# A fused four-stage kernel: the embedding product on four column groups, edge transfers in GpSimd's queue, and two coefficient loads earlier in SP's queue

## The chip, the core and the metric

The kernel runs on one core of a Trainium2 chip, as one program with one launch. The core has five engines that run side by side, each through its own instructions in order: TensorE (PE in the profile, PEld for its weight loads), VectorE (DVE), ScalarE (ACT), GpSimd (POOL) and SyncE (SP). SP, ScalarE and GpSimd can each issue DMA transfers (SPq, ACTq, POOLq in the trace). The metric is the time of one execution on the device in microseconds (us); lower is better. Before the change the median of three runs is 2675.97 us (2674.63 to 2677.31).

## What is computed

The input `x` is a batch of 8 matrices of 512 x 512 in float32. Four layers follow each other; the diff touches the first and the start of the second.

```python
# layer 0, per batch: a stencil with given coefficient grids
gradv_Af  = grad(A[0]*f, 0) + grad(A[1]*f, 1)
gradvv_Bf = grad2(B[0]*f, 0) + grad2(B[1]*f, 1) + grad(grad(B[2]*f, 1), 0) + grad(grad(B[2]*f, 0), 1)
x = max(f + (-gradv_Af + gradvv_Bf * 0.5) * dt, 0)
# layer 1: attention, 16 heads of 32, with an adaptive layer norm
emb = silu(sin_emb(timestep)) @ W_ada + b_ada          # [8, 512] @ [512, 1024]
scale, shift = split(emb, 2)
x = ln(x) * (1 + scale) + shift
q, k, v = x @ Wq + bq, x @ Wk + bk, x @ Wv + bv
scores = q / sqrt(32) @ k.T + attention_bias, masked; probs = softmax(scores)
x = x + (probs @ v) @ Wo + bo
x = x + ff(ln(x) * g2 + beta2)
# layer 2: per batch one of 8 experts (gelu MLP, residual, norm)
# layer 3: low-rank response with a gate
```

## The kernel before

**Stages.** `fused_kernel` builds the constants and the silu of the sine embedding `sc` (128 partitions, 4 chunks, 8 batches). Then `grid_stage` does layer 0 for the first batch alone. `attention_stage` loops over 8 batches x 4 chunks x 4 row blocks ("units"); while it attends over batch b it also does layer 0 of batch b + 1, in small steps that it spreads over the units (`grid_loads`, `grid_step`, `grid_early`). `mlp_stage` does the rest. Nearly every instruction is pinned (`keep_in_program_order`, called `pin`), so on each engine the order in the code is the order on the chip. A matrix of 512 rows lies as 128 partitions x 4 row blocks (R = 4).

**The first batch's grid stage.** SP loads A, B, `f` and the weights. VectorE makes the coefficient grids and products; PE adds them up with shifted identities (`zi`) into four PSUM accumulators `acc[r]`, one for each row block (called `l0_r`, tile `l`, L251). The first and last row of the matrix have their own formulas. They are computed apart, on 64 partitions, into `xe` (blocks of 16 partitions: side x batch, for all 8 batches). The six coefficient grids are stored to DRAM through GpSimd's queue (L405: `coef_q`, `e`, `g`, `c`, `a`, `b`, 1 MB each) so that later batches can load them.

**The tail of the grid stage**, which the change touches:
- `embed(ps)` (L138 to 148): the product of `W_ada` and `sc`. Each of the 8 output chunks takes 4 matmuls with a 128x128 block of `wada` as the stationary operand and 8 columns of `sc` moving. The result `pe` lies as [128, 8, 8].
- Four steps on VectorE (L248, called from L514) take `acc[r]` to `x[:, r]`, in the order r = 0, 3, 1, 2, each followed by a Relu on ScalarE (L515).
- `edges()` (L501 to 513) runs after the Relu of r = 3. It overwrites the first and the last row of `x` from `xe`, in four transfers: two for the first row on SP's queue and two for the last row on ScalarE's.
- Four transfers on ScalarE's queue (L520) store all of `xe` to DRAM as `xed`, for the later batches.
- `stats(1)`, `stats(2)`, `stats(0)`, `stats(3)` on VectorE (L523, L524): statistics by row block. Row block 0 holds the first row of the matrix, row block 3 the last. Then the inverse root on GpSimd (L532) and four normalising steps on VectorE (L535).
- `embed_out(pe)` (L157): adds the bias and gives `ada`, the scale and shift.

**The head of the attention stage** is written out by hand from L1119 on. SP's queue gets: the mask of row block 0 (`mask_in`, L588), `grid_loads(1, -2)` (the second batch's `f` as `gf`, L713 to L718, and two q coefficients, L706), the first unit's bias (two transfers of 512 KB, L995), `Wv`, `grid_loads(1, -1)` (coefficients e and c, 512 KB each, L706), the next mask, the second unit's bias, `Wo`. On PE come the transposes of the first batch (`x1_in`, tile `xtr`, L570), the first q and k blocks (`pq`, `pk`, L567), the first scores (`s`), the v blocks (`pv`), and from then on a mix of units. Between the units VectorE does the products of the second batch's stencil (`gv`, L689), the softmax maximum with the bias (`bt`, L1030), and the sum of `bo` (L581). GpSimd adds the mask to the bias (L1006). ScalarE does the exponentials (L1035).

**Completion counters.** The tile framework gives each DMA one of eight completion counters in turn. SP's and ScalarE's transfers share one set of eight, GpSimd's have another set. A transfer waits until the one that had its counter before, eight transfers back in the same set, has landed. So in SP's queue L588 waits for the first edge transfer, and L717 for the third store of `xed`.

Of the kernel before, what the change touches and what calls it, by code (L numbers as in the profile page):

```python
# [11 lines left out]
F32 = mybir.dt.float32  # L12
# [4 lines left out]
ALU = mybir.AluOpType  # L17
# [3 lines left out]
NB = 8  # L21
S = 512
D = 512
P = 128
# [5 lines left out]
KC = D // P  # L30
RK = 32
# [8 lines left out]
def fused_kernel(ctx: ExitStack, tc: tile.TileContext, a: dict):  # L40
    nc = tc.nc

    const = ctx.enter_context(tc.tile_pool(name="const", bufs=1))
    small = ctx.enter_context(tc.tile_pool(name="small", bufs=4))
# [3 lines left out]
    ident = const.tile([P, P], F32, name="ident")  # L48
    make_identity(nc, ident)
    mhalf = const.tile([P, R], F32, name="mhalf")  # L50
# [4 lines left out]
    ada = const.tile([P, 2 * KC, NB], F32, name="ada")  # L55
# [4 lines left out]
    def x_home(b):  # L60
        return xp.tile([P, R, D], F32, name=f"x{b}", tag=f"x{b % 4}", bufs=1)

    xt = {0: x_home(0)}
# [10 lines left out]
    def layernorm(dst, src, eps, tag, pin=lambda i: i):  # L74
# [17 lines left out]
    wada = [  # L92
        xp.tile([P, KC, D], F32, name=f"wada{h}", tag=f"x{2 + h}", bufs=1) for h in range(2)
    ]
# [14 lines left out]
    bada = ep.tile([P, 2 * KC], F32, name="bada")  # L109
# [18 lines left out]
    sc = ep.tile([P, KC, NB], F32, name="sc")  # L128
# [6 lines left out]
    nc.scalar.activation(sc[:, 2:4, :], ang, AF.Sin)  # L135
    nc.scalar.activation(sc, sc, AF.Silu)

    def embed(ps):  # L138

        pe = ps.tile([P, 2 * KC, NB], F32, name="pe")  # L140
        for m in range(2 * KC):
            o = (m % KC) * P
            for k in range(KC):
                tc.keep_in_program_order(
                    nc.tensor.matmul(  # L145
                        pe[:, m, :], lhsT=wada[m // KC][:, k, o : o + P], rhs=sc[:, k, :],
                        start=k == 0, stop=k == KC - 1,
                    )
                )
        return pe  # L150

    def embed_bias():
# [4 lines left out]
    def embed_out(pe):  # L157
        tc.keep_in_program_order(
            nc.vector.tensor_tensor(
                ada, pe, bada[:, :, None].to_broadcast([P, 2 * KC, NB]), ALU.add  # L160
            )
        )

    dram = ctx.enter_context(tc.tile_pool(name="x1_dram", bufs=1, space=bass.MemoryType.DRAM))
# [13 lines left out]
    def load_rows():  # L178
# [5 lines left out]
        nc.sync.dma_start(bo, a["bo"][None, :].to_broadcast([P, D]))  # L184

    grid = grid_stage(
        tc, a, const, small, dram, xt[0], mhalf, ident, load_wada, load_w, load_rows, embed,
        embed_bias, embed_out,
    )


# [29 lines left out]


def grid_stage(
    tc, a, const, small, dram, x, mhalf, ident, load_wada, load_w, load_rows, embed,
    embed_bias, embed_out,
):


# [12 lines left out]
    nc = tc.nc  # L241
    pin = tc.keep_in_program_order
# [10 lines left out]
    with ExitStack() as ctx:  # L253
        cp = ctx.enter_context(tc.tile_pool(name="coef", bufs=1))
        gp = ctx.enter_context(tc.tile_pool(name="edge", bufs=1))
        ps = ctx.enter_context(tc.tile_pool(name="l0_ps", bufs=1, space=PSUM))
# [14 lines left out]
        n, W = 2 * NB, 128  # L271
# [11 lines left out]
        with tc.tile_pool(name="raw", bufs=1) as rp:  # L283
            a0, b0, a1, b1 = (
                rp.tile([P, R, D], F32, name=k) for k in ("a0", "b0", "a1", "b1")
            )

            ec8 = rp.tile([N // NB, 12, W + 2], F32, name="ec8")
            sel8 = rp.tile([N // NB, N // NB, NB], F32, name="sel8")
            pin(nc.gpsimd.memset(ec8, 0.0))  # L290

            def edge_cols(k):
                lo, hi = max(0, W * k - 1), min(D, W * k + W + 1)
                return slice(lo, hi), slice(lo - W * k + 1, hi - W * k + 1)

            for i, k in enumerate(blocks):
                c, u = edge_cols(k)
                pin(nc.gpsimd.dma_start(ec8[2 * i : 2 * i + 2, :, u], a["edge_c"][:, :, c]))
            pin(
                nc.gpsimd.tensor_copy(  # L300
                    sel8, ident[0 : N // NB, 0 : N // NB, None].to_broadcast([N // NB, N // NB, NB])
                )
            )

            halves = slice(0, 2), slice(2, 4)
            for h in halves:
                rows_in(b1, a["B"][1], h)
                rows_in(a1, a["A"][1], h)
            rows_in(b0, a["B"][0])
            rows_in(a0, a["A"][0])  # L310
            rows_in(f, a["x"][0])
            rows_in(b2, a["B"][2])
            nc.sync.dma_start(gw, a["c_ghost"].to_broadcast([P, 16]))
            nc.sync.dma_start(dth, a["dt"][None, :].to_broadcast([P, NB]))
            load_wada()
            load_w("Wq", "Wk")
            load_rows()
            pin(nc.gpsimd.memset(zi, 0.0))
            pin(nc.gpsimd.tensor_copy(zi[:, 0, 1 : P + 1], ident))
            pin(nc.gpsimd.tensor_scalar_mul(zi[:, 1, 1 : P + 1], ident, -1.0))  # L320
            gate = small.tile([P, 1], F32, name="gate_e", tag="gate_e", bufs=1)
            pin(nc.gpsimd.tensor_tensor(gate, f[:, 0, 0:1], f[:, 0, 0:1], ALU.add))
            for i, k in enumerate(blocks):
                c, u = edge_cols(k)
                pin(nc.gpsimd.dma_start(fe[n * i : n * i + n, :, u], a["edge_f"][:, :, c]))

            for i in range(4):
                pec = ps.tile([N, 3, W + 2], F32, name=f"pec_{i}", tag="pec", bufs=2)
                mm(
                    pec, sel8.rearrange("q s b -> q (s b)"), ec8[:, 3 * i : 3 * i + 3, :],  # L330
                    True, True,
                )
                pin(nc.scalar.copy(ec[:, 3 * i : 3 * i + 3, :], pec))

            for h in halves:
                tt(ca[:, h, :], b1[:, h, :], a1[:, h, :], ALU.add)
                tt(cb[:, h, :], b1[:, h, :], a1[:, h, :], ALU.subtract)
            tt(cc, b0, b1, ALU.add)
            pin(nc.scalar.mul(cc, cc, -2.0))
            tt(ce, a0, b0, ALU.add)  # L340
            tt(cg, b0, a0, ALU.subtract)
            pin(nc.scalar.mul(b2, b2, 0.5))
# [34 lines left out]
        for i, (u, v) in enumerate(  # L377
            ((ga[:, :, 1:5], gb[:, :, 0:4]), (gb[:, :, 508:512], ga[:, :, 509:513]))
        ):
            for k, w in enumerate((u, v)):  # L380
                o = 8 * i + 4 * k
# [100 lines left out]
        for p, i in ends:  # L482
            cols = (slice(1, 5), slice(W - 3, W + 1))[i]
            for k in range(2):
                o = 8 * i + 4 * k
# [7 lines left out]
        xe = cp.tile([N, W], F32, name="xe")  # L493
        stt(xe, se, dte, fe[:, 0, C], ALU.mult, ALU.add)
        pin(nc.vector.tensor_scalar(xe, xe, 0.0, None, ALU.max))
        pe = embed(ps)
        embed_bias()
        pin(nc.vector.tensor_scalar(dth, dth, 0.5, None, ALU.mult))
        st = small.tile([P, R, 6], F32, name="ln0_st", tag="ln0_st", bufs=1)
        mv = small.tile([P, R, 2], F32, name="ln0_mv", tag="ln0_mv", bufs=1)  # L500
        def edges():  # L501
            for o, u, c in ((0, 3 * n, 0), (n, n, 2 * W)):
                for side, q_ in ((0, nc.sync), (1, nc.scalar)):
                    p, r = side * (P - 1), side * (R - 1)
                    e0 = o + side * NB
                    pin(
                        q_.dma_start(
                            x[p : p + 1, r, c : c + 2 * W].rearrange("o (b w) -> o b w", w=W),
                            xe[e0 : e0 + u + 1 : u, :],
                        )  # L510
                    )
# [5 lines left out]
                edges()  # L517
        xed = dram.tile([n, D], F32, name="xed")
        for i, k in enumerate(blocks):
            pin(nc.scalar.dma_start(xed[:, W * k : W * k + W], xe[n * i : n * i + n, :]))  # L520

        def stats(r):
            pin(nc.vector.bn_stats(st[:, r, :], x[:, r, :]))  # L523
            pin(nc.vector.bn_aggr(mv[:, r, :], st[:, r, :]))  # L524

        stats(1)
        stats(2)
        stats(0)
# [16 lines left out]
def attention_stage(  # L545
# [12 lines left out]
    nc = tc.nc  # L558
    with ExitStack() as ctx:
        wp = ctx.enter_context(tc.tile_pool(name="aw", bufs=1, reuse_waits="tile"))  # L560
        pp = ctx.enter_context(tc.tile_pool(name="ap", bufs=2, reuse_waits="tile"))
        ps = ctx.enter_context(tc.tile_pool(name="a_ps", bufs=1, space=PSUM, reuse_waits="tile"))

        pin = tc.keep_in_program_order
# [156 lines left out]
        def grid_loads(n, j):  # L721
            if j == -2:
                xt[n] = x_home(n)
                grid_f(n)
            for k, key, p in (
                (-2, "q", 0), (-2, "q", 1), (-1, "e", 0), (-1, "c", 0), (1, "g", 0), (2, "a", 0),
                (4, "b", 0), (4, "q", 2), (6, "e", 1), (7, "c", 1), (8, "g", 1), (9, "a", 1),
                (10, "b", 1),
            ):
                if j == k:  # L730
                    coef(n, key, p)
# [258 lines left out]
        def load_bias(b, c, r):  # L990
            for u in range(2):
                hp = 2 * c + u
                bt = pp.tile([P, 2, S], F32, name=f"bt_{b}_{r}_{hp}", tag="bt", bufs=8)
                pin(
                    nc.sync.dma_start(  # L995
                        bt,
                        a["bias"][b, 2 * hp : 2 * hp + 2].rearrange("h (p r) k -> r p h k", r=R)[r],
                    )
                )
                bias[b, c, r, u] = bt  # L1000
# [119 lines left out]
        n = len(units)  # L1120
        mask_in(0, 0)
        grid_loads(1, -2)
        load_bias(*units[0])
        load_w("Wv")
        grid_loads(1, -1)
        mask_in(0, 1)
        load_bias(*units[1])
        load_w("Wo")
# [949 lines left out]
```

## Time and profile before

| what | us |
|---|---|
| median of 3 runs (lowest, highest) | 2675.97 (2674.63, 2677.31) |
| the profiled execution | 2674.74 |
| its span, first to last instruction | 2673.0 |
| PE busy in 0 to 60 / 60 to 100 / 100 to 200 / 200 to 1000 / 1000 to 2673 | 42.52 / 39.22 / 95.39 / 799.51 / 1660.26 |
| embedding product, L145, on the chain that ended last | 9.52 |
| first transposes of the attention stage, `xtr`, start on that chain | 59.62 |
| first softmax step of the first unit on DVE (L1030) starts | 77.74 |

The profile is one execution taken by the hardware profiler; durations that are quoted from it belong to that execution. A timeline row gives start, length, engine, line, operation, output <- input, count, and in brackets how long the engine had been idle and what ended it. A DMA row shows when the transfer was issued, not when it landed. PE's busy time is no measure of distance from its peak, since matmuls are pipelined.

Small transfers and their times from issue to landing, in the profile's list of DMA issues: `fe` 5.6 and 5.3 us, `ec` 6.0 and 6.4, the 2 KB rows of `coef_q` 3.8, the 1 MB stores `coef_q` to `coef_b` 4.3 to 12.5 (all in GpSimd's queue). For SP's and ScalarE's queues it lists no such times.

### The profile page before, as it was taken

How to read it: one execution, taken by the hardware profiler on the slowest of the kernel's cores; microseconds unless marked ns; L12 is line 12 of the kernel's file. 1: busy time of each engine (PE TensorE's matmuls, PEld its weight loads, DVE VectorE, ACT ScalarE, POOL GpSimd, SP SyncE). 2: the span in 40 equal slices, each digit the busy share in tenths (PEclk: the TensorE clock that was granted, in tenths of full speed). 3: DMA queues.
4: the chain of work that ended last, by engine and by line, in shares of the span. 5: the costliest groups of instructions: out<-in, count | busy, mean ns of one | idle time of the engine just before them, and what ended most of it. 6: DMA issues, size and time to landing. Idle time of an engine off the chain costs nothing.

```text
span 2673.0 us, 39423 instructions
## 1 busy us (share of the span) xinstructions
PE 2636.9 (99%) x14182; PEld 1958.2 (73%) x14182; DVE 1885.6 (71%) x3444; ACT 1004.4 (38%) x2091; POOL 1479.3 (55%) x1091
## 2 busy tenths in 40 slices
PE   7999999999999999999999999999999999999998
PEld 4455555555555555888888888888888888888887
DVE  7888898888888656676656656656566676676675
ACT  2576767677777765211211211211111221221221
POOL 3456565556555654565566565655535545545543
PEclk9999999999999999999999999999999999999999
DMA  8775766666666554653544454445335445445331
GB/s 313 262 239 192 249 211 228 212 246 235 204 238 221 186 169 148 197 147 85 162 148 122 141 150 143 118 135 171 107 128 184 132 148 185 133 147 185 123 105 38
DMA packets 241760, 460.31 MB, mean 172 GB/s; under 512 B 33848, under 2 KB 77440, under 8 KB 232478
## 3 DMA queue, kind: packets, MB, share of 16 engines
q1 hardware_dynamic: 237754, 447.04, 49.3%
q0 software_dynamic: 3360, 10.68, 2.9%
q8 instruction: 113, 1.85, 0.3%
q14 instruction: 81, 0.66, 0.1%
q10 hardware_dynamic: 452, 0.07, 0.0%
HBM read 398.43 MB, written 55.09 MB: 170 GB/s over the span
## 4 chain that ended last, share of the span: by engine, by line
PE 96%; DVE 2%; DMA 1%; ACT 0%; issue 0%; SPq 0%; POOL 0%; DVEq 0%; POOLq 0%; ACTq 0%
PE u L1221 29%; PE y L1221 29%; PE tr L570 9%; PE s L567 6%; PE ctx L567 4%; PE pv L567 4%; PE o L567 4%; PE pk L567 4%; PE pq L567 4%; PE l L251 1%; PE xtr L570 1%; PE xb L570 1%; DVE bt L1030 0%; DMA a<-in_A 0%; PE po L1221 0%; PE pe L145 0%
## 5 line engine op out<-in xcount | busy, mean ns | idle before, releaser
L1006 POOL TENSOR_TENSOR bt<-bt,mk 128x1024 f32<-128x1024 f32 x256 | 541.0, 2138 | 70.4 <-DMA bt<-in_bias 63.6
L1221 PE MATMUL y<-wo,act 128*128 128x256 f32 x2560 | 566.3, 380 | 0.0
L1221 PEld LDWEIGHTS y<-wo,act 128*128 128x128 f32 x2560 | 484.5, 190 | 71.6 <-issue 6.7
L1035 ACT ACTIVATE bt<-bt,mn 128x512 f32<-128x512 f32 x512 | 365.7, 718 | 84.9 <-DVE mn L1030 84.8
L570 PEld LDWEIGHTS tr<-ident,bt 128*128 128x128 f32 x2048 | 229.5, 141 | 148.0 <-issue 100.6
L1030 DVE CUSTOM_DVE_ANT_0 bt<-s,bt 128x512 f32<-128x512 f32 x512 | 330.2, 683 | 3.8 <-PE s L567 3.6
L1221 PE MATMUL u<-bt,wi 128*128 128x256 f32 x1440 | 330.5, 379 | 0.0
L1227 DVE TENSOR_TENSOR act<-u,u 128x512 f32<-128x512 f32 x256 | 173.1, 683 | 200.7 <-PE u L1221 129.7
L1221 PEld LDWEIGHTS u<-bt,wi 128*128 128x128 f32 x1440 | 273.5, 190 | 37.2
L570 PE MATMUL tr<-ident,bt 128*128 128x128 f32 x2048 | 277.0, 278 | 6.1 <-DVE pt L1060 1.7
L1062 ACT COPY pt<-tr 128x512 f32<-128x512 f32 x368 | 203.9, 584 | 207.5 <-PE tr L570 202.2
L1221 PE MATMUL u<-tb,ws 128*128 128x256 f32 x1024 | 242.2, 379 | 0.0
L1221 PE MATMUL y<-t,s 128*128 128x256 f32 x1024 | 227.8, 380 | 0.0
L1230 POOL TENSOR_TENSOR t<-wo,t 128x512 f32<-128x512 f32 x64 | 107.4, 1701 | 203.0 <-PE y L1221 203.0
L1221 PEld LDWEIGHTS u<-tb,ws 128*128 128x128 f32 x1024 | 194.3, 190 | 26.6 <-DVE tb L1227 0.2
L1221 PEld LDWEIGHTS y<-t,s 128*128 128x128 f32 x1024 | 194.0, 190 | 26.1
L1060 DVE COPY pt<-tr 128x512 f32<-128x512 f32 x144 | 99.2, 689 | 139.9 <-PE tr L570 139.0
L1585 ACT ACTIVATE act<-act,b 128x512 f32<-128x512 f32 x128 | 82.9, 711 | 292.7 <-DVE act L1227 292.7
L1585 ACT ACTIVATE act<-act,bi 128x512 f32<-128x512 f32 x128 | 83.8, 712 | 282.6 <-DVE act L1227 282.6
L1604 ACT COPY u<-u 128x512 f32<-128x512 f32 x64 | 36.4, 569 | 393.8 <-PE u L1221 277.5
L1227 DVE TENSOR_TENSOR x<-y,x 128x512 f32<-128x512 f32 (+1 forms) x97 | 64.7, 680 | 153.9 <-PE y L1221 103.6
L1227 DVE TENSOR_TENSOR u<-u,u 128x512 f32<-128x512 f32 x192 | 130.9, 682 | 55.4 <-PE u L1221 55.3
(324 smaller groups left out, 4191.1 us busy)
## 6 DMA issues: line engine op xcount, KB each, us to landing
bt<-in_bias SPq DMA_DIRECT2D x256, 512.0 KB
wo<-in_W SPq DMA_DIRECT2D x32, 1024.0 KB
wi<-in_Wi SPq DMA_DIRECT2D x32, 1024.0 KB
wo<-in_Wo_e SPq DMA_DIRECT2D x32, 1024.0 KB
wi<-in_W SPq DMA_DIRECT2D x28, 1024.0 KB
td<-tt SPq DMA_DIRECT2D x22, 1024.0 KB
bt<-td SPq DMA_DIRECT2D x176, 128.0 KB
gq<-coef_q SPq DMA_DIRECT2D x21, 512.0 KB
```

The lines of the kernel that those rows point to most:

```text
L567: pin(nc.tensor.matmul(out, lhsT=lhsT, rhs=rhs, start=start, stop=stop))
L570: pin(nc.tensor.transpose(out, src, ident))
L1006: nc.gpsimd.tensor_tensor(bt, bt, mask[b, r][:, None, :].to_broadcast([P, 2, S]), ALU.add)
L1030: nc.vector.tensor_tensor_reduce(bt[:, i, :], ss[h], bt[:, i, :], -1.0, 3.0e38, ALU.add, ALU.min, mn)
L1035: nc.scalar.activation(bt[:, i, :], bt[:, i, :], AF.Exp, bias=mn, scale=-1.0, accum_out=sums[b, c][:, h, r : r + 1],)
L1060: pin(nc.vector.tensor_copy(pt[:, :, r % 2, :], tr))
L1062: pin(nc.scalar.copy(pt[:, :, r % 2, :], tr))
L1221: pin(nc.tensor.matmul(out, lhsT=lhsT, rhs=rhs, start=start, stop=stop))
L1227: pin(nc.vector.tensor_tensor(out, x, y, op))
L1230: pin(nc.gpsimd.tensor_tensor(out, x, y, op))
L1585: nc.scalar.activation(acts[g][:, k, :], acts[g][:, k, :], func, bias=bi[:, j : j + 1])
L1604: pin(nc.scalar.copy(u1, p[0]))
```

## The change

There are three parts.

1. The embedding product turns its operands round. `sc` is put into a zeroed tile `sp` of 32 columns for each chunk (8 of them used), which is the stationary operand. `W_ada` streams through as the moving operand in pieces of 256 columns, and the four pieces go to four groups of 32 output partitions. The result `rows` is [4 x 32, 256], with the batch along partitions; ScalarE copies it to SBUF, and PE turns it back with two transposes. `embed_out` reads the turned layout.
2. The two transfers of the last row (`edges()`, side 1) and the four stores of `xed` are issued by GpSimd instead of ScalarE.
3. In the attention stage's head, `grid_loads(1, -1)` (e and c coefficients) goes ahead of the first bias and `Wv`.

```diff
+    def embed_in(pool):
+        sp = pool.tile([P, KC, RK], F32, name="sp")
+        tc.keep_in_program_order(nc.gpsimd.memset(sp, 0.0))
+        tc.keep_in_program_order(nc.gpsimd.tensor_copy(sp[:, :, 0:NB], sc))
+        return sp
+
-    def embed(ps):
-        pe = ps.tile([P, 2 * KC, NB], F32, name="pe")
-        for m in range(2 * KC):
-            o = (m % KC) * P
-            for k in range(KC):
-                tc.keep_in_program_order(
-                    nc.tensor.matmul(
-                        pe[:, m, :], lhsT=wada[m // KC][:, k, o : o + P], rhs=sc[:, k, :],
-                        start=k == 0, stop=k == KC - 1,
-                    )
-                )
-        return pe
+    def embed(ps, sp):
+        pin = tc.keep_in_program_order
+        rows = ps.tile([P, 2 * P], F32, name="pe_rows", tag="pec", bufs=2)
+        for k in range(KC):
+            for j in range(4):
+                o = 2 * P * (j % 2)
+                pin(
+                    nc.tensor.matmul(
+                        rows[j * RK : (j + 1) * RK, :], lhsT=sp[:, k, :],
+                        rhs=wada[j // 2][:, k, o : o + 2 * P], start=k == 0, stop=k == KC - 1,
+                    )
+                )
+        return rows
+
+    def embed_turn(ps, pool, rows):
+        er = pool.tile([P, 2 * P], F32, name="pe_sb")
+        tc.keep_in_program_order(nc.scalar.copy(er, rows))
+        pe = ps.tile([P, 2, P], F32, name="pe", tag="pec", bufs=2)
+        for h in range(2):
+            tc.keep_in_program_order(
+                nc.tensor.transpose(pe[:, h, :], er[:, h * P : (h + 1) * P], ident)
+            )
         return pe
...
     def embed_out(pe):
         tc.keep_in_program_order(
             nc.vector.tensor_tensor(
-                ada, pe, bada[:, :, None].to_broadcast([P, 2 * KC, NB]), ALU.add
+                ada.rearrange("p (j h) b -> p j h b", h=2),
+                pe.rearrange("p h (j b) -> p j h b", j=4)[:, :, :, 0:NB],
+                bada.rearrange("p (j h) -> p j h", h=2)[:, :, :, None].to_broadcast([P, 4, 2, NB]),
+                ALU.add,
             )
         )
...
             pin(nc.gpsimd.tensor_scalar_mul(zi[:, 1, 1 : P + 1], ident, -1.0))
+            sp = embed_in(gp)
             gate = small.tile([P, 1], F32, name="gate_e", tag="gate_e", bufs=1)
...
-        pe = embed(ps)
+        pe = embed(ps, sp)
...
-                for side, q_ in ((0, nc.sync), (1, nc.scalar)):
+                for side, q_ in ((0, nc.sync), (1, nc.gpsimd)):
...
-            pin(nc.scalar.dma_start(xed[:, W * k : W * k + W], xe[n * i : n * i + n, :]))
+            pin(nc.gpsimd.dma_start(xed[:, W * k : W * k + W], xe[n * i : n * i + n, :]))
...
+        pe = embed_turn(ps, gp, pe)
         stats(1)
...
         grid_loads(1, -2)
+        grid_loads(1, -1)
         load_bias(*units[0])
         load_w("Wv")
-        grid_loads(1, -1)
         mask_in(0, 1)
```

More of the change, by code (lines that the diff above doesn't have):

```diff
@@ L186, in fused_kernel @@
     grid = grid_stage(
-        tc, a, const, small, dram, xt[0], mhalf, ident, load_wada, load_w, load_rows, embed,
-        embed_bias, embed_out,
+        tc, a, const, small, dram, xt[0], mhalf, ident, load_wada, load_w, load_rows, embed_in, embed,
+        embed_turn, embed_bias, embed_out,
     )
@@ L223, in grid_stage @@
 def grid_stage(
-    tc, a, const, small, dram, x, mhalf, ident, load_wada, load_w, load_rows, embed,
-    embed_bias, embed_out,
+    tc, a, const, small, dram, x, mhalf, ident, load_wada, load_w, load_rows, embed_in, embed,
+    embed_turn, embed_bias, embed_out,
 ):
```

## The prediction

> **What bounds the kernel now.** I read the page first: its busy shares, then the chain that ended last.
>
> ```profile
> span 2673.0 us, 39423 instructions
> PE 2636.9 (99%) x14182; PEld 1958.2 (73%) x14182; DVE 1885.6 (71%) x3444; ACT 1004.4 (38%) x2091; POOL 1479.3 (55%) x1091
> PE 96%; DVE 2%; DMA 1%; ACT 0%; issue 0%; SPq 0%; POOL 0%; DVEq 0%; POOLq 0%; ACTq 0%
> ```
>
> TensorE (PE) sets the end. Time is won or lost only where PE's start in some stretch moves, or where PE waits. Everything the diff touches lies in the first 100 us, so next comes the chain of waits from 46 to 75 us (start, length, what):
>
> ```profile
> 45.81 4.29 PE l L251 x10
> 50.11 9.52 PE pe L145 x64
> 59.62 3.51 PE xtr L570 x16
> 63.13 4.20 PE pq L567 x8
> 67.33 3.45 PE pk L567 x8
> 70.80 0.70 ACT kt L658
> 71.54 1.14 PE s L567 x8
> 72.68 2.34 PE pv L567 x5
> ```
>
> The embedding product (L145) stands on the chain with 9.52 us; the transposes of the first batch (xtr) follow at once. Third, the timeline of the same stretch, for what else xtr needs: the normalised x.
>
> ```profile
> 49.21 0.63 ACT L515 ACTIVATE x<-x 128x512 f32<-128x512 f32 x1 [0.23 <-DVE x L248]
> 49.88 1.81 ACTq L507 DMA_DIRECT2D x<-xe  x2
> 51.73 0.63 ACT L515 ACTIVATE x<-x 128x512 f32<-128x512 f32 x1 [1.88 <-DMA x<-xe]
> 52.39 0.69 DVE L523 BATCH_NORM_STATS2 ln_st<-x 128x6 f32<-128x512 f32 x1 [1.50 <-ACT x L515]
> 52.62 0.34 SPq L588 DMA_DIRECT2D mu<-in_mask  x1
> 54.82 0.67 DVE L523 BATCH_NORM_STATS2 ln_st<-x 128x6 f32<-128x512 f32 x1
> 57.09 1.92 DVE L535 TENSOR_SCALAR x<-x,ln_mv,ln_r 128x512 f32<-128x512 f32 x4 [1.17 <-POOL ln_r L532]
> 58.79 0.22 SPq L717 DMA_DIRECT2D gf<-in_x  x1
> ```
>
> x is normalised at 57.09 + 1.92 = 59.01, only 0.6 us before PE finishes the embedding. Two chains run side by side and almost tie; shortening one alone is worth 0.6.
>
> **The embedding product.** 64 instructions of 8 columns go. In come 16 matmuls of 32 output rows and 256 columns, two records each: exactly the form of ctx (L567), whose 32 records take 1.86 us in the chain. So the product ends at 50.11 + 1.86 = 51.97. Then come ScalarE's copy of 128x256 (nearest row: 64x390, 0.48) and two transposes (four of tr take 0.66, so 0.33); with some 0.1 of hand-over PE is done at 52.9. DVE's add of the bias (0.22) still stands behind the normalisation. If the four column groups did not overlap, 32 records at the old 256 ns each would be 8.2 and PE done at 59.2, which is still before 59.62. Now the cover is gone and the normalisation decides: with its old end plus 0.04, xtr starts at 59.05, a gain of 0.6. POOL's two new instructions (clearing and filling sp) lie in its 11.08 us wait before L322 and cost nothing; without that wait they would cost two small POOL operations, 0.3 each by the zi rows.
>
> The new hole on PE, 52.9 to about 58.5, bears on its clock. The granted clock was already 0.58 at 54 to 56 us and 0.50 from 56 to 64, although PE shows itself busy, and 1.00 from 66. I take the hole at nothing: xtr starts at half clock in both. Bounds: were xtr and pq at full clock, xtr would be about 2.1 (eight tr take 1.03) and pq 3.43, so -2.2; were pk at half, about +1.7 (half of the 3.45 again).
>
> [...]
>
> **The edge DMAs.** ScalarE now does its four Relus without issuing two transfers in between. The third (51.73) can start when the third of four L248 steps ends, 47.57 + 3 x 0.83 = 50.1, so the first statistics start at 50.9 instead of 52.39, the second at 51.7. The next, of row block 0, needs SP's two edge transfers. SP's L588 waited 1.4 us for the first of them until 52.62, and L713, which stands behind the second, went at 53.14; so 53.1, and the last statistics 0.81 later (54.01 to 54.82 in the trace) at 53.9 at the earliest. That last one, row block 3, needs the two transfers that now go through POOL's queue. They are issued when the second Relu ends, 49.84, at about 0.5 each (POOL's issue rows are 0.49 to 0.59), the second at 50.4. POOL's transfers took from 3.8 us (the 2 KB rows of coef_q) to 5.6 (the 32 KB ones of fe) from issue to landing. So 54.2 to 56.0. From 54.82 to 59.01 is 4.19; hence xtr at 54.2 + 4.19 + 0.04 = 58.4 to 60.2, against 59.62: -1.2 to +0.6. I take -1.2: 1 KB out of SBUF is nearest to the 2 KB row. It contains the embedding's 0.6. POOL then issues four xed stores (2 us, to about 53) before the power of the variance (56.00 before); that queue is free in time.
>
> [...]
>
> SP's own queue gains: in the built order the mask load L588 no longer waits for an edge transfer, and L717 no longer for the xed store (3.0 us in SP's waits). So the load of f for the second batch goes at about 51.5, not 53.14, and the q coefficients some 3 us before 59.39. The DMA share was 0.17 in 52 to 54 and 0.19 in 59 to 60: the holes get filled, about 3 us of transfer.
>
> **The e and c coefficients.** Two loads of 512 KB pass the first bias pair, Wv and a mask. At the 404 to 408 GB/s of 66 to 72 us these 1.05 MB take 2.6, so Wv lands 2.6 later by this alone. It had landed by 70.93 (SP's L995 waited 0.4 for it), and pv began at 72.68. With xtr 1.2 earlier, pv wants it at 71.5: 70.93 + 2.6 - 3 = 70.5, no wait; without those 3 us it is a wait of 2.0. I take 0, range 0 to +2.0. The bias adds on POOL (67.05) likewise stay about where they are.
>
> What is won: VectorE stood idle 6.18 us before 72.22 for coef_e, and its first softmax step came at 77.74 though the scores were ready at 72.7.
>
> ```profile
> 72.22 1.22 DVE L689 TENSOR_TENSOR x<-x,gf 128x1024 f32<-128x1024 f32 x1 [6.18 <-DMA x<-coef_e]
> 95.62 0.69 DVE L581 TENSOR_TENSOR bo<-pb,bo 128x512 f32<-128x512 f32 x1
> 104.72 2.35 PE L567 MATMUL s<-kt,qt 32*128 32x512 f32 x8
> ```
>
> But PE runs without a break in the chain from 72.68 to 102.17; no PE instruction there asks for what VectorE had late. Where PE does wait for VectorE, from 102 on, VectorE's run of work begins at 95.62 with a sum that needs pb, which PE ended at 92.15 + 3.44 = 95.59. VectorE had caught up there before. Its lead is lost in a wait for pb, and the order of its instructions does not change. So 0 on the path. Other end: PE idles 2.16 us in 100 to 130 and 2.45 in 130 to 200, and three score groups (104.72, 112.37, 118.31) take 2.35 instead of 1.14, 3.6 in all: at most -8.2.
>
> **Sum.** -1.2 + 0 + 0. The profiled execution took 2674.74 around its span of 2673.0; it becomes 2673.5. The median of the runs is 1.23 above that execution, so 2674.8.
>
> **Rivals.**
> - VectorE's lead does reach PE. For it: 6.18 us of idle go, and PE's waits between 102 and 122 name VectorE. Against: the 95.62 row. If the 2.16 and the 3.6 go, with -1.2: 2669.0.
> - The POOL edges land late, slower than before. For it: coef_b, issued at 40.23 in the same queue, took 12.5 us behind five other 1 MB stores. Against: the DMA share falls to 0.17 at 52, the stores are through. With 12.5: 50.4 + 12.5 + 4.23 = 67.1, +7.5, so 2683.5. It decides from a landing of 5.0 us on (no gain), and beyond 0.2% from 10.3.
> - Wv late: +2.0 - 1.2, 2676.8. For it the two loads ahead; against it the two holes.
> - The column groups don't overlap: -0.4 (59.2 instead of 59.62), 2675.6.
>
> **How the numbers follow.** Forecast 0.62 (own range 2672 to 2677: the edge and clock bounds), VectorE's lead 0.16, POOL late 0.07, Wv late 0.12, no overlap 0.03. Within 0.2% (5.35 us, about what a measurement of this kernel can tell from no change) lie 2670.6 to 2681.3. Faster: 0.16, and 0.03 of the forecast where clock and waits add up: 0.19. Slower: 0.07 and 0.02 of Wv late with a cold pk: 0.09. Same: 0.72. The range must take in Wv late and most of what lies toward the first rival: 2670.0 to 2679.0.
>
> **What would show it.** Right: L153 about 1.9 us; xtr starting at 58 to 59; the last statistics waiting for DMA x<-xe; L740 not waiting for xed; pv not waiting for Wv; coef_e landed before VectorE asks; bo still waiting for pb. Wrong: xtr after 60; pv waiting more than 1 us; or the waits of PE between 102 and 122 gone.

## The result, and the profile after

| | us |
|---|---|
| changed kernel, median of 22 runs (lowest, highest) | 2680.29 (2676.61, 2684.40) |
| kernel before, 22 runs beside them | 2675.52 (2672.41, 2679.62) |
| time after / time before, 95% interval | 1.0015 (1.0009 to 1.0021) |
| the profiled execution after: time, span | 2684.40, 2682.6 |

The change costs some 4 to 5 us. The forecast was 2674.8 with a range up to 2679.0; the median lies above it. The profiled execution is the longest of the 22, so its lengths are read place by place, and the sizes of effects come from the medians. Lines behind the embedding functions are numbered 21 to 23 higher than before (L567 is now L590, L171 is L192).

From the page of the changed kernel: the span, the busy shares, one DMA queue (packets, MB, share), and the shares of the chain that ended last.

```profile
span 2682.6 us, 39373 instructions
...
PE 2632.7 (98%) x14152; PEld 1949.1 (73%) x14152; DVE 1885.6 (70%) x3444; ACT 1004.5 (37%) x2092; POOL 1481.3 (55%) x1099
...
q8 instruction: 113, 1.85, 0.3%
...
PE 92%; DMA 3%; DVE 2%; ACT 1%; SPq 1%; issue 0%; POOL 0%; DVEq 0%; POOLq 0%; ACTq 0%
```

PE has 4 us less to do (2632.7 against 2636.9), and the span is 9.6 longer: PE waits more. On the chain DMA has 3% where it had 1%. The queue called "instruction" will matter below; the prediction has no word on it.

The timeline of PE in the changed kernel, 50 to 75 us (start, length, idle time before and what ended it):

```profile
50.04 1.93 PE L153 MATMUL pe_rows<-wada,sp 128*32 128x256 f32 x32
52.46 0.44 PE L166 MATMUL pe<-ident,pe_sb 128*128 128x128 f32 x2 [0.49 <-ACT pe_sb L162]
57.42 4.10 PE L593 MATMUL xtr<-ident,x 128*128 128x128 f32 x16 [4.52 <-issue]
61.35 3.60 PE L590 MATMUL pq<-x,Wq 128*128 128x512 f32 x8
64.79 3.60 PE L590 MATMUL pk<-x,Wk 128*128 128x512 f32 x8
69.17 1.14 PE L590 MATMUL s<-kt,qt 32*128 32x512 f32 x8 [0.78 <-ACT kt L681]
74.91 2.05 PE L590 MATMUL pv<-Wv,x 128*128 128x512 f32 x2 [4.61 <-DMA Wv<-in_Wv]
```

The product, xtr and pq went well: `s` starts 2.4 us earlier than before (69.17 against 71.54). Then `pv` waits 4.61 us for Wv and starts 2.2 later than before. The chain of waits of the changed kernel says what Wv hung on:

```profile
53.67 7.91 DMA gf<-in_x
...
61.59 0.32 SPq L729
...
63.22 11.56 DMA Wv<-in_Wv
...
74.91 5.30 PE pv L590 x8
```

SP's queue stood for the second batch's `f` (`gf`), and Wv, issued at 63.22 (61.25 before), took 11.56 us to land. That is the first half of the story. The timeline of VectorE begins as forecast:

```profile
50.81 0.68 DVE L545 BATCH_NORM_STATS2 ln_st<-x 128x6 f32<-128x512 f32 x1
...
53.05 0.69 DVE L545 BATCH_NORM_STATS2 ln_st<-x 128x6 f32<-128x512 f32 x1 [0.54 <-DMA x<-xe]
54.46 0.69 DVE L545 BATCH_NORM_STATS2 ln_st<-x 128x6 f32<-128x512 f32 x1 [0.51 <-DMA x<-xe]
...
56.75 1.93 DVE L558 TENSOR_SCALAR x<-x,ln_mv,ln_r 128x512 f32<-128x512 f32 x4 [1.17 <-POOL ln_r L555]
...
68.09 1.23 DVE L712 TENSOR_TENSOR x<-x,gf 128x1024 f32<-128x1024 f32 x1 [1.94 <-DMA x<-coef_e]
...
99.52 0.69 DVE L604 TENSOR_TENSOR bo<-pb,bo 128x512 f32<-128x512 f32 x1 [3.06 <-PE pb L590]
```

VectorE had e 4.1 us earlier (68.09 against 72.22), but its first softmax step starts at 77.47 against 77.74: the lead is gone by then. Between the two stand two small products of the stencil's edge columns (`m`), 2.09 us each where they took 0.17. In the changed kernel, then in the kernel before, with GpSimd's first two additions of mask and bias (67.05):

```profile
71.50 2.09 DVE L769 TENSOR_TENSOR m<-gab,gf 128x16 f32<-128x16 f32 x1
...
73.61 2.09 DVE L769 TENSOR_TENSOR m<-gab,gf 128x16 f32<-128x16 f32 x1
```

```profile
67.05 4.20 POOL L1006 TENSOR_TENSOR bt<-bt,mk 128x1024 f32<-128x1024 f32 x2 [9.69 <-DMA bt<-in_bias]
...
75.63 0.17 DVE L746 TENSOR_TENSOR m<-gab,gf 128x16 f32<-128x16 f32 x1
```

The later bias moves GpSimd's additions to 70.96 to 75.67 us, on top of the two products. All five kernels with e and c ahead of the bias show the same pair, 2.09 to 2.10 us each; the twelve others have 0.17 with these additions over. The 3.06 us at `bo` are a wait for PE's `pb`, which is late behind `pv`.

### The profile page after: what moved, and what is told of

Read it like the earlier page. It is cut to its first block, busy times and chain, and to the rows that moved or that the text cites. A ratio compares the mean times of both kernels' runs of the same rounds, so it can differ in the third digit from the quotient of the medians.

```text
span 2682.6 us, 39373 instructions
## 1 busy us (share of the span) xinstructions
PE 2632.7 (98%) x14152; PEld 1949.1 (73%) x14152; DVE 1885.6 (70%) x3444; ACT 1004.5 (37%) x2092; POOL 1481.3 (55%) x1099
## 3 DMA queue, kind: packets, MB, share of 16 engines
q8 instruction: 113, 1.85, 0.3%
## 4 chain that ended last, share of the span: by engine, by line
PE 92%; DMA 3%; DVE 2%; ACT 1%; SPq 1%; issue 0%; POOL 0%; DVEq 0%; POOLq 0%; ACTq 0%
PE u L1244 29%; PE y L1244 27%; PE tr L593 8%; PE s L590 5%; PE ctx L590 4%; PE pv L590 4%; PE o L590 4%; PE pk L590 4%; PE pq L590 4%; PE l L272 1%; DMA td<-tt 1%; DVE bt L1053 1%; DMA bt<-td 1%; PE xb L593 1%; DMA a<-in_A 0%
## 5 line engine op out<-in xcount | busy, mean ns | idle before, releaser
L590 PE MATMUL s<-kt,qt 32*128 32x512 f32 x1024 | 169.5, 643 | 0.8 <-ACT kt L681 0.8
```

The lines of the kernel that those rows point to most:

```text
L590: pin(nc.tensor.matmul(out, lhsT=lhsT, rhs=rhs, start=start, stop=stop))
```

## The experiments

Every row is a median over the runs of one kernel and over those of the kernel before in the same session. An interval of 0.09% to either side is 2.4 us, so single differences of 1 us are not secured, and only rows whose interval leaves out 1 are told from no change. The ratio is not the quotient of the two medians: for b_shift it stands for 3.2 us where the medians give 4.5, for wv_pad for -1.1 where they give -2.9.

| run | time | kernel before | difference | ratio (95%) |
|---|---|---|---|---|
| e1_embed: product alone | 2678.53 | 2675.43 | +3.1 | 1.0012 (1.0003 to 1.0022) |
| e2_edges: edge transfers alone | 2675.85 | 2675.43 | +0.4 | 1.0003 (0.9994 to 1.0012) |
| e3_order: order of the loads alone | 2678.26 | 2675.43 | +2.8 | 1.0011 (1.0002 to 1.0020) |
| e4_embed_edges: product and edges | 2678.46 | 2675.43 | +3.0 | 1.0015 (1.0006 to 1.0024) |
| e4_pad: the same, refills put back | 2673.24 | 2675.57 | -2.3 | 0.9991 (0.9982 to 1.0000) |
| after_pad: whole change, refills put back | 2675.23 | 2675.57 | -0.3 | 0.9997 (0.9988 to 1.0006) |
| b_shift: kernel before, refills shifted | 2680.03 | 2675.57 | +4.5 | 1.0012 (1.0003 to 1.0020) |
| e4_warm: e4 with the hole filled | 2673.19 | 2675.57 | -2.4 | 0.9991 (0.9982 to 1.0000) |
| e1_pad: product alone, refills put back | 2673.66 | 2676.29 | -2.6 | 0.9994 (0.9985 to 1.0003) |
| e4_mid: put back from 163 us on | 2675.60 | 2676.29 | -0.7 | 0.9994 (0.9985 to 1.0003) |
| e4_late: put back from 1069 us on | 2677.09 | 2676.29 | +0.8 | 1.0001 (0.9992 to 1.0010) |
| wv_pad: Wv first, refills put back | 2673.36 | 2676.29 | -2.9 | 0.9996 (0.9987 to 1.0005) |
| b_256: kernel before, one whole refill more | 2677.14 | 2676.49 | +0.7 | 1.0001 (0.9992 to 1.0010) |
| b_128: kernel before, half a refill more | 2677.20 | 2676.49 | +0.7 | 1.0002 (0.9993 to 1.0011) |
| wv_warm: Wv first, hole filled | 2678.17 | 2676.49 | +1.7 | 1.0000 (0.9991 to 1.0009) |

**The parts, one by one.** The first theory was that the order of the loads alone does the harm. e1_embed has the new product in the kernel before (all of the diff's `embed_in`, `embed`, `embed_turn`, `embed_out`), e4_embed_edges that and the edges. The other two are short:

```diff
# e2_edges
-                for side, q_ in ((0, nc.sync), (1, nc.scalar)):
+                for side, q_ in ((0, nc.sync), (1, nc.gpsimd)):
...
-            pin(nc.scalar.dma_start(xed[:, W * k : W * k + W], xe[n * i : n * i + n, :]))
+            pin(nc.gpsimd.dma_start(xed[:, W * k : W * k + W], xe[n * i : n * i + n, :]))
# e3_order (e4_embed_edges is the changed kernel with these lines as before)
         grid_loads(1, -2)
+        grid_loads(1, -1)
         load_bias(*units[0])
         load_w("Wv")
-        grid_loads(1, -1)
```

> The kernel before with the embedding product on four column groups alone; both the edge transfers and the order of the loads are the old ones. Before took 2675.5 us by the median of 22 runs. Theory T (the loss comes from Wv, which lands late because e and c of the second batch stand ahead of it): PE is done with the product near 53, the normalisation then decides as it did (its end was 59.01), so xtr starts at about 59.0, pv does not wait for Wv, and the time is 2674 to 2676. Rival R (the loss comes from the edge and xed transfers in GpSimd's queue): the same, 2674 to 2676. Rival C (the new hole of 4 to 5 us on PE is what costs, through a slower granted clock afterwards): 2678 to 2681, with xtr, pq or pk longer than before (3.51, 4.20 and 3.45 us).

> The kernel before with the edge and xed transfers in GpSimd's queue alone. Theory T: the embedding product still holds PE until 59.6, pv does not wait for Wv by more than 0.5 us, and the time is 2674.5 to 2676.5. Rival R: the load of f for the second batch goes out early and mixes with the stores, the coefficients and Wv land late, pv waits more than 1 us for Wv, and the time is 2677 to 2681. Rival C: as T.

> The kernel before with e and c of the second batch loaded ahead of the first bias pair and Wv, alone. Theory T: Wv lands 2.5 to 6 us later than in the kernel before (where it had landed by 70.9), pv waits 1 to 4 us for it, the granted clock falls after that wait, and the time is 2677 to 2681. Rival R: no wait for Wv of more than 0.5 us, time 2673 to 2676.5. Rival C: as R.

> The changed kernel without its third part: e and c of the second batch stand behind Wv again. Theory T: pv does not wait for Wv by more than 0.5 us, xtr starts near 57.4 and s near 69.2 as in the changed kernel, and the 2.4 us that the changed kernel had gained up to s are kept: 2672 to 2674.5. Rival R: pv waits more than 1 us for Wv, and the time is 2677 to 2681, as that of the changed kernel (2680.3). Rival C: no wait, but a longer pq, pk or pv, and 2677 to 2681.

e3_order does cost 2.8 us, the time that theory T gave, but without its sign: in its profile, the shortest of its 11 runs, pv waits 0.68 us for Wv where T had 1 to 4. What the order alone costs there is open. e2_edges costs nothing that can be told from none, so rival R falls. But T expected the product to be free, and it costs 3 us with the edges and without them. Rival C's time came true for e1 and e4, and a part of its sign: xtr takes 4.33 and 4.35 us (3.65 before), and pq 4.68 in e4 (4.41 before). But `s` starts at 70.88 and 70.69, earlier than the old 71.54, so nothing is lost up to there; and e4_pad, below, has the same hole and an xtr of 4.12 and is fast. Another cause had to be found.

What the profiles of the three kernels with the new product (after, e1, e4) shared lay far from the product: PE waits in the last stage, which none of the kernels with the old product had. And the trace's packets of the queue "instruction" had moved. Queue q8 brings 113 packets of 16 KB (1.85 MB in all). Between two of them PE starts 256 instructions on average (255.9 in the profile before, 255.5 after; single gaps 158 to 338). From this the author reads the packets as refills of PE's own instruction stream, of 256 instructions, which makes 64 bytes each (an estimate: 16 KB over 256); the trace does not name the engine that a packet is for. They are called refills below. PE has 29,084 instructions in the trace before and 29,025 after: 59 fewer (60 matmul and weight-load instructions fewer, one wait more). In the author's reading each refill behind the new product then comes 59 instructions later in the code. Start of the q8 packets from 30 us on, us:

```
before      52.2   84.2  114.4  132.9  154.2
after       52.2   98.6  121.9  147.3  159.6
after_pad   39.9   81.4  112.3  131.3  152.2
b_shift     53.7   94.8  118.0  143.8  158.5
b_256       52.7   84.2  114.1  134.1  155.9
```

What the runs below put back is, in this reading, the place of a refill in the code; its start can still lie elsewhere (in e1_pad the second one starts at 94.6).

**Putting the refills back, and shifting them where nothing else changed.** PE stands idle for 12.6 us at the start. Small matmuls there are instructions that cost no time on the path (in e4_pad 30 records took 0.90 us, and PE then still waited 10.34 us for `ec`); their results are not used.

```diff
# e4_pad, after_pad: 15 (60 instructions); b_shift: 49 (196 = 256 - 60), in the kernel before
             for i in range(4):
                 pec = ps.tile([N, 3, W + 2], F32, name=f"pec_{i}", tag="pec", bufs=2)
+                for _ in range(15 if i == 0 else 0):
+                    mm(pec[0:8, 0, 0:8], ident[0:8, 0:8], ident[0:8, 0:8], True, True)
# e4_warm: 60 instructions of full width in PE's new hole, behind the embedding's transposes
+        for _ in range(15):
+            tc.keep_in_program_order(
+                nc.tensor.matmul(rows[:, 0:P], lhsT=ident, rhs=ident, start=True, stop=True)
+            )
```

> The changed kernel without its third part, with 15 matmuls of 8 columns ahead of everything else on PE, where it stands idle for 12.6 us: 60 instructions, as many as the new embedding product has fewer. Theory F (the new product makes PE's instruction stream 59 instructions shorter; its 16 KB refills then fall elsewhere in the later loops, into short DMA round trips that others wait for): the refills come back to the places of the kernel before (near 84, 114, 133 and 154 us), VectorE does not wait for rbs near 160, PE does not wait for bt in the last stage, and the 2.4 us gained up to s are kept: 2672 to 2674.5, against 2678.5 without the 15. Theory G (the loss of this kernel is in its hole on PE and the clock, or in the data's transfers): 2677.5 to 2679.5, as without them.

> The kernel before with 49 such small matmuls in the same idle place: 196 instructions more, which puts the refills 60 instructions later in the code (196 = 256 - 60; a refill brings 16 KB, 256 instructions of 64 bytes), where the new embedding product puts them. Nothing else differs. F: refills near 95, 118, 137 and 158 us, VectorE waits 0.2 to 1 us for rbs near 160, PE waits for bt in the last stage once or more, and the time is 2677 to 2679. G: no effect, 2674.5 to 2676.5.

> The whole change with the 15 small matmuls. F: the refills are back where they were, what stays is the wait of pv for Wv: 2676 to 2678.5, against 2680.3. G: 2679 to 2681.5.

> The changed kernel without its third part, with 15 matmuls of 128x128 columns in PE's new hole, right behind the two transposes of the embedding (about 3.3 us of full use in a hole of 5.0, and 60 instructions, so the refills lie as in the kernel before). [...] With F: 2670.5 to 2673. F without the clock: 2672 to 2674.5. Clock without F: 2675.5 to 2677.5. Neither: 2677.5 to 2679.5.

In the ranges of e4_warm "the clock" stands for the author's estimate that with the hole filled xtr takes about 2.1 us in place of the 4.35 of e4_embed_edges and pq 3.6 in place of 4.68. All four go the way of theory F, in both directions: 5.2 us come back in e4 and 5.1 in the whole change (medians), and the unchanged kernel loses 4.5. Two lie outside its ranges: b_shift at 2680.0 (2677 to 2679) and after_pad at 2675.2 (2676 to 2678.5). The clock is no rival: at equal mean clock b_shift takes 2681.1 against 2676.9 us (0.995, 5 and 9 runs) and 2677.1 against 2674.8 (0.996, 3 and 6 runs). Not every sign came: in e4_pad VectorE did wait for rbs near 160 (1.70 us), with the refill at 152.2, so that wait comes without a refill beside it too; and in b_shift PE did not wait for bt in the last stage. In e4_warm the clock stayed at 1.00 from 52 to 70 us (0.50 from 58 to 62 in e4_embed_edges), xtr took 2.98 us, pq 3.60, and `s` came at 68.12, 1 us before e4_pad (69.09), but the total is the same: PE then waited 1.5 us for `bo`.

**Where in the kernel the shift costs.** The 15 small matmuls go into a wait of PE later on, or ahead of the product alone.

```diff
# e4_mid, in turned(), PE's wait near 163 us
+                if (b, c, r, u, i) == (0, 2, 1, 1, 1):
+                    pad = ps.tile([P, S], F32, name="pad", tag="m")
+                    for _ in range(15):
+                        mm(pad[0:8, 0:8], ident[0:8, 0:8], ident[0:8, 0:8], True, True)
# e4_late: the same 15 between the two halves of the last o_block(NB - 1, 0), PE's wait near 1069 us
# e1_pad: e1_embed with the 15 at the start
```

> The kernel before with the new embedding product alone, and the 15 small matmuls in PE's idle start, so that the refills stand where the kernel before has them. F (all of what the product alone cost, 3.1 us, came from the shifted refills): 2674 to 2676. If a part of it came from the hole on PE or from the clock: 2677 to 2679.

> The changed kernel without its third part, with the 15 small matmuls not at the start but in PE's wait near 163 us: up to there the refills stand shifted, behind it as in the kernel before. If what the shift costs (5.2 us, 2678.5 against 2673.2) arises before 163: 2677.5 to 2679.5. If it arises behind: 2672.5 to 2674.5. In between: in proportion.

> The same with the 15 small matmuls in PE's wait near 1069 us, ahead of the last stage. If what the shift costs arises in the last stage (PE's waits for bt there, 0.7 us in the profile of the kernel without them, and none in that of the kernel with them at the start): 2672.5 to 2674.5. If it arises in the attention: 2677.5 to 2679.5. From the profiles I expect some 1 to 1.5 us from the last stage, so 2677 to 2677.5.

e1_pad takes 2673.7, a little under F's 2674 to 2676: all that the product alone had cost comes back. From e4 to e4_late to e4_mid to e4_pad the difference to the kernel before goes +3.0, +0.8, -0.7, -2.3: the cost is spread, some 2 us in the last stage and the rest on both sides of 163 us (by the ratios 3.7, 1.9 and 0.8). With intervals of 2.4 us the trend is shown, not each share. In the last stage one place can be seen where a refill and the end of a store come together. In e4_embed_edges, 2006.0 to 2012.2 us, the DMA view (GB/s in 40 steps, then the refill's queue):

```profile
GB/s 238 277 211 119 185 277 370 330 462 502 515 396 449 436 423 423 423 423 423 423 423 423 239 470 282 380 274 278 185 161 81 29 40 40 13 13 13 26 13 0
...
q8 instruction: 1, 0.02, 0.9%
```

The store `td` moves at 423 GB/s in the middle of this stretch and ends in a tail of 13 to 40. One 16 KB refill took 0.94 us (2009.95 to 2010.89), and behind it the last 2 KB packets come one after another until 2012.04. What held them is not shown; the trace does not name a packet's DMA engine. SP's queue waits for the store before it issues the loads `bt`; SP's waits in e4_embed_edges, then at the same place in the kernel before, then in e4_late (total, times, longest):

```profile
SPq L1488 <- DMA td<-tt: 7.7, 1, 7.7
```

```profile
SPq L1465 <- DMA td<-tt: 6.5, 1, 6.5
```

```profile
SPq L1494 <- DMA td<-tt: 6.6, 1, 6.6
```

SP waits 1.1 to 1.2 us longer with the refill there, in one profile of each kernel. What PE makes of it in e4_embed_edges from 1100 to 2640 us:

```profile
PE pf L1244 <- ACT bt L1758: 0.7, 2, 0.4
```

The kernels after and e1_embed have this wait too (1.2 us in four, 0.3 in one); no kernel with the refills in their old places has it. That is the one such place seen, and PE's waits for `bt` come to 0.7 us in e4; the refills moved in b_shift make no such wait, and yet it loses 4.5. That the rest of the cost arises in the same way was the author's estimate from the times of the runs; it is not shown.

**Is it the place or the number of instructions?** b_256 and b_128 are b_shift with 64 and 32 small matmuls.

> The kernel before with 64 of the small matmuls in PE's idle start: 256 instructions, one whole refill, so all later refills stand in the same places of the code as before (near 84, 114, 133, 154 us). If the place of the refills decides: 2674.5 to 2676.5, as before. If the added instructions or the additional refill cost something (as in the kernel with 49, 2680.0): 2678 to 2681.

> The kernel before with 32 of them: 128 instructions, half a refill, so that later refills stand half way between the old places. If the place decides, the time is another one than with 64, but which I cannot say beforehand: 2674 to 2680, with PE's waits in the last stage for bt present or absent by where the refills fall. If added instructions cost: 2677 to 2679, between none and 49.

256 instructions more, in this reading one refill more, cost nothing that can be told from none; 196 cost 4.5. So it is no price for each instruction; in the author's reading the place decides. Neither came as forecast. b_256 lies between its two ranges, beside a kernel before that took 2676.5 in that session. b_128 was to differ from b_256 if the place decides, and does not; its time alone would fit a price for each instruction, but then 256 would have to cost twice as much, and they cost the same. 128 instructions more cost nothing that can be told from none here (+0.7), so in this reading it is particular places that hurt, and which ones no run says beforehand.

**Another order.** wv_pad issues Wv, then e and c, then the first bias pair; wv_warm has the full-width matmuls in the hole in place of the 15 at the start.

```diff
         grid_loads(1, -2)
+        load_w("Wv")
         grid_loads(1, -1)
         load_bias(*units[0])
-        load_w("Wv")
```

> The changed kernel with Wv ahead of e and c, these ahead of the first bias pair, and the 15 small matmuls at the start. Wv is then no later than without the third part, and VectorE gets e and c some 3 us earlier than there: PE waits neither for Wv nor for bo, s near 69, pv near 70.2: 2671 to 2673.5. If the late bias pair makes the softmax wait instead: 2674 to 2677.

> The changed kernel with Wv ahead of e and c, these ahead of the first bias pair, and 15 matmuls of 128x128 columns in PE's new hole in place of the small ones at the start. With the hole filled, s comes near 68.1 (as in the kernel with them and without the third part) and pv follows at 69.2 with no wait for Wv, and VectorE has e and c in time for bo: 2670 to 2672.5, against 2673.4 with the small ones. If Wv or the bias pair then comes too late: 2673 to 2675.

wv_pad, within its range, is as good as e4_pad and e1_pad, not better. wv_warm missed by 3 us or more. Its PE timeline:

```profile
67.96 1.14 PE L594 MATMUL s<-kt,qt 32*128 32x512 f32 x8 [0.78 <-ACT kt L685]
...
95.36 3.70 PE L594 MATMUL pk<-x,Wk 128*128 128x512 f32 x8 [2.49 <-DVE bo L608]
```

`s` came 3.6 us earlier than in the kernel before, and 2.5 of it were lost in a wait for `bo`: VectorE had e at 67.37 and reached `bo` only at 94.62 (72.22 and 95.62 before). VectorE ran without a listed wait in between, 27.25 us in place of 23.40; the difference of 3.85 is the two small products of 2.10 us each, which again run beside GpSimd's additions (70.67 to 74.96). The best that was measured are e4_pad and e4_warm, 0.9991 of the time before with an interval that ends at 1: the product and the edges without the new order, and 60 instructions that put the refills back.

## Why the prediction failed, step by step

In the terms of its own sum (medians against the kernel before): product and edges -2.3 where -1.2 stood (e4_pad), the order of the loads +2.0 where 0 stood (after_pad less e4_pad), and +5.1 for which there was no term (after less after_pad). Together +4.8. From the spread of the runs each of the last two is uncertain by about 2 us, so the +2.0 is not told from none; the order alone cost +2.8 (e3_order).

- **The failing step: "64 instructions of 8 columns go. In come 16 matmuls".** It priced their durations and ended with PE "done at 52.9", which is exact (52.46 + 0.44). It did not ask what fewer instructions do to the rest of PE's stream. No rival had it either, although the page has the row "q8 instruction: 113, 1.85, 0.3%" before and after. With the refills put back the whole change takes 2675.2, with the forecast of 2674.8 within its interval; that is partly luck, since -2.3 and +2.0 stand there for -1.2 and 0. What the shifted refills run into is seen at one place only (SP's wait of 7.7 us for `td` in place of 6.5).
- **The second: "70.93 + 2.6 - 3 = 70.5, no wait".** One of its own signs of being wrong came, pv waiting more than 1 us. The 3 us of "holes get filled" did not come. The f load did go out early (51.76, forecast "about 51.5"), but the stretch behind it moved less per us, not more. Windows of 58 to 66 us (window, length, PE busy, clock, DMA share, GB/s) in the kernel before, the changed kernel, and after_pad:

```profile
58.00:60.00 2.00, 2.00 (x11) 0.50 0.61 185
60.00:62.00 2.00, 2.00 (x11) 0.50 0.72 173
62.00:64.00 2.00, 2.00 (x8) 0.50 0.97 368
64.00:66.00 2.00, 2.00 (x5) 0.86 0.90 263
```

```profile
58.00:60.00 2.00, 2.00 (x8) 0.50 0.74 233
60.00:62.00 2.00, 2.00 (x11) 0.72 0.41 131
62.00:64.00 2.00, 2.00 (x6) 1.00 0.92 221
64.00:66.00 2.00, 2.00 (x6) 1.00 0.73 166
```

```profile
58.00:60.00 2.00, 2.00 (x10) 0.50 1.04 325
60.00:62.00 2.00, 2.00 (x8) 0.59 1.02 317
62.00:64.00 2.00, 2.00 (x6) 1.00 0.85 309
64.00:66.00 2.00, 2.00 (x6) 1.00 1.03 405
```

  In after_pad pv waits 0.90 us for Wv, in the changed kernel 4.61, in e3_order 0.68 (its profiled execution was the shortest of its 11). The rival "Wv late" named the right wait. That its +2.0 is what after_pad less e4_pad gives is no support by itself, since only 0.90 us of it stand at pv. Of the +5.1 between after_pad and the changed kernel 3.7 stand at pv in these two profiles, the changed kernel's being the longest of its 22. Why its transfers behind 57 us were slower is open. The refill at 52 us does not settle it: after, e4 and e4_warm have one and move 131 to 303 GB/s in 58 to 64 us, after_pad and e4_pad have none and move 309 to 384, but wv_warm has one and moves 316 to 362, and e1_pad has none and moves 167 to 363.
- **The cold clock behind such a wait** was named ("Wv late with a cold pk") but at the wrong matmul: at pv's wait the clock fell to 0.50 for 6.83 us (from 71.37 on), and pv took 15.60 us against 14.00.
- **Right: the edge DMAs.** Statistics at 50.81, 53.05 and 54.46 where the text has 50.9, 53.1 and "54.2 to 56.0"; GpSimd's two transfers took 3.9 us to land, where it had chosen 3.8. The mis-sized term is xtr's start: 57.42, not 58.4. "That old end plus 0.04" took xtr to wait for all four normalising steps, while the transposes of the first row block run behind the first of them, as the new trace shows (xtr starts 0.67 us into the 1.93). The edges alone are worth nothing (+0.4, not told from none).
- **Right in the number, not in the reason: VectorE's lead is worth 0 on the path.** "Its lead is lost in a wait for pb" is not what happened. "The bias adds on POOL (67.05) likewise stay about where they are" failed: they went to 70.96, and VectorE's lead was lost beside them, 3.8 us in two small products, before its first softmax step. e also came later than the text has it: VectorE still waited 1.94 us for it. PE's short waits between 102 and 122 us are all there. What the lead would be worth without the two long products no run shows. The same tie works the other way: where PE comes earlier (e4_warm, wv_warm), it waits for `bo`.
- **Right within its bounds: the clock.** The half clock at 54 us lasted 6.83 us in place of 10.24; pq took 3.60 in place of 4.41, but xtr 4.10 in place of 3.65. From the start of xtr to the start of pk it is 7.37 us in place of 7.69: a gain of 0.3 where 0 stood with a bound of -2.2.

## What to carry to other kernels

Here an edit took 59 instructions out of PE's stream; in this kernel, which is tuned to fractions of a per cent, their absence cost more than the edit won (+5.1 against -2.3), in the author's reading because PE's instruction refills shifted against everything behind them. Before a small loss is explained from the edited place, put the number of instructions back with idle ones, and shift the unchanged kernel by the same amount: two cheap runs that tell the edit from its displacement. Where two engines tie (PE and VectorE at `bo`), count the gain of one only up to the other, and a load that is moved ahead counts as a delay for what it passes, whatever holes are expected to be filled. Ask also what the delayed load releases on a third engine, and what that will then run beside: here GpSimd's additions, beside two products of VectorE.

## What the runs showed of the hardware that was not expected

**The granted clock fell behind waits of 1.7 to 4.1 us, and not behind every one.** In 17 profiles the half-clock stretches (leaving out the end of the kernel) last 3.41, 6.83 or 10.24 us, 12, 23 and 4 times: one, two or three times 3.41. In the profile of the kernel before they begin at 54.30 and 1057.82 us, 294 times 3.413 us apart; in e1_embed the first begins at 56.26. 14 of the 17 profiles have a half-clock stretch that begins between 163 and 171 us, behind a wait of 1.7 to 4.1 us, in 12 of them 3.1 or less. The timeline of PE there in e4_embed_edges, then in the kernel before:

```profile
164.57 0.66 PE L593 MATMUL tr<-ident,bt 128*128 128x128 f32 x4 [1.98 <-DVE x L633]
165.17 0.66 PE L593 MATMUL xtr<-ident,x 128*128 128x128 f32 x4
165.76 2.70 PE L590 MATMUL s<-kt,qt 32*128 32x512 f32 x8
168.38 3.64 PE L590 MATMUL ctx<-pt,v 128*32 128x256 f32 x32
```

```profile
164.59 0.66 PE L570 MATMUL tr<-ident,bt 128*128 128x128 f32 x4 [1.69 <-DVE x L610]
165.19 0.66 PE L570 MATMUL xtr<-ident,x 128*128 128x128 f32 x4
165.78 1.75 PE L567 MATMUL s<-kt,qt 32*128 32x512 f32 x8
167.46 1.93 PE L567 MATMUL ctx<-pt,v 128*32 128x256 f32 x32
```

The same instructions after nearly the same wait; one execution pays 2.7 us more in `s` and `ctx` than the other. Its clock was 0.50 from 168 to 172 us; in the kernel before it was 1.00 there. In e2_edges and e3_order the wait is 1.68 us in both, and `s` takes 2.70 us in the first and 1.75 in the second. What decides it is not shown. Runs with a lower mean clock are the longer ones: the 33 runs of the kernel before beside e1_embed have a mean time of 2677.6 us at a mean clock of 0.994 (3 runs) and of 2674.2 at 0.997 (8 runs).

**A packet of the queue "instruction" beside the end of a store.** The 16 KB packet at 2010 us took 0.94 us; of 16 x 6.2 us that is the 0.9% that the view gives for it. All 113 of them together are 0.3% of the DMA engines' time; yet SP waited 1.1 to 1.2 us longer for the store that had this one in its last stretch (7.7 us against 6.5 and 6.6).

**VectorE's small product took 2.09 us beside an addition of GpSimd.** In the 17 profiles the product `m` of 16 elements a partition took 0.16 to 0.17 us 228 times, and 2.09 to 2.10 us the ten times that it ran beside one of GpSimd's additions of 1024 elements; in all ten it ends 0.03 to 0.05 us after the addition does (73.59 and 73.56 in the changed kernel). It goes the other way too: in the five kernels with the new order the first addition begins while VectorE still multiplies 1024 elements, 0.20 to 0.64 us before that product ends, and takes 2.18 to 2.62 us in place of 2.13. That the two engines wait for each other is the author's reading of these rows; why they would is not shown.
